# Taking row maxima off attention scores by 32-row products instead of 64-row products

## The chip, the cores and the metric

The kernel runs on one core of a Trainium2 chip. The metric is the device time of one execution in microseconds (us). TensorE does the matrix products, VectorE (DVE) the reductions, ScalarE (ACT) the exponentials, GpSimd (POOL) small elementwise work and indirect DMA, and SyncE (SP) issues most transfers. All numbers are float32.

## The reference

The input x is 2 sequences of 2048 tokens with 256 features. The reference is one attention layer, a layer norm, one mixing and mixture-of-experts layer, and a layer norm:

```
qkv = x @ qkv_w + qkv_b            # 16 heads of 16; q and k rotated by a table indexed by head
scores = einsum('bhqd,bhkd->bhqk', q, k) / 16 ** 0.5
out = einsum('bhqk,bhkd->bhqd', softmax(scores), v) @ out_w + out_b
x = layernorm(x + out)
n = layer_norm(x, g1, be1);  x = x + n + (n @ mix_w + mix_b)
n = layer_norm(x, g2, be2)
probs = softmax(n @ router_w);  combine = weights of the 2 best of 8 experts
y_e = silu(n @ w1[e] + b1[e]) @ w2[e] + b2[e]
x = layernorm(x_before_ffn + sum_e combine_e * y_e)   # layernorm adds its own input too
```

The change concerns the second line and the softmax: every row of scores has its maximum subtracted before the exponential.

## The kernel before

**Stages.** A leading stage (to about 95 us) makes q, k and v of the first sequence. The attention stage follows, to about 1720 us by the trace. The experts' products fill the rest: tokens are gathered in lists by expert and worked on in tiles of 256.

**Visits and steps.** Attention is a list of 32 visits `w`: 2 sequences, 4 blocks of 512 queries, 4 groups of 4 heads. A visit has 16 steps `kt`, one for each 128 keys, so there are 512 steps. A step handles 128 keys by 512 queries for 4 heads.

**Operands.** A head has only 16 features. To keep precision, q and k are split in a high and a low part, and the four combinations are stacked: one head takes 64 partitions (16 features by 4 parts). Tiles `km[w][pair]` and `qm[w][pair]` hold two heads each, one in partitions 0 to 63, the other in 64 to 127. A product of one head therefore uses 64 rows of the 128-row array, and two heads stand side by side in the array: the profile shows such products as form 64*128 (rows by columns). They run in pairs, at the same time.

**One step.** TensorE's instructions stand in the order in which the program issues them (`tc.manual_schedule` covers TensorE, ScalarE, VectorE and SyncE):

1. `scores(w, kt, 0)` and `scores(w, kt, 1)`: for each of the two pairs of heads, two score products (line 529) into two PSUM banks of the pool `ps_sc` (4 banks), then two products (line 538) that add minus the row maximum to the same banks. The maxima of all 4 heads are rows of `mrow[w]`, each as a high and a low part; `sel[pair]` is a 0/1 matrix that picks the two rows of a head. Both line-538 products have 64 rows, nearly all zeros. Four exponentials (line 544) follow on ScalarE, one for each bank.
2. `max_step(t + AHEAD, 0)`: half of the row maxima's work for a step that comes 18 steps later (`AHEAD`). `maxima` makes two score products of 64 rows (line 485), transposed, into banks of the pool `ps_mx`, and VectorE reduces each to a column of maxima (line 493). `ps_mx` has 3 banks, so each product needs the bank that was used three products before, and waits until VectorE has reduced that one.
3. `values` of the step before: 4 heads times 128*32 products (line 559), side by side in the array's columns. One such group appears as 8 matmul records, in two passes.
4. `work(1.0)`: a queue of small jobs, due by step number and not by time: projections of finished blocks, the router, the q, k and v of the second sequence, copies of finished outputs.
5. `max_step(t + AHEAD, 1)`: the second half of the maxima's work, two more line-485 products.

In the last 18 steps nothing is left for `maxima`, and items 2 and 5 are empty.

**After a visit's maxima.** `maxima_done` puts the 4 heads' maxima, as high and low parts, in 8 columns of `mt`; `rows_of` transposes that into `mrow[w]`. `make_sel` makes the selecting matrices once, in the leading stage.

Of the kernel before, what the change touches and what calls it, by code (L numbers as in the profile page):

```python
# [24 lines left out]
F32 = mybir.dt.float32  # L25
F32R = mybir.dt.float32r
I32 = mybir.dt.int32
AF = mybir.ActivationFunctionType
# [4 lines left out]
P = 128  # L33
# [30 lines left out]
def seq_postln_kernel(  # L64
# [16 lines left out]
    nc = tc.nc  # L81
# [7 lines left out]
    ident = cp.tile([P, P], F32, name="ident")  # L89
# [63 lines left out]
    with ExitStack() as actx:  # L153

        ep = actx.enter_context(tc.tile_pool(name="early", bufs=1))
        ap_ = actx.enter_context(tc.tile_pool(name="attn", bufs=1))
        dp = actx.enter_context(tc.tile_pool(name="stacks", bufs=1, space=bass.MemoryType.DRAM))
        ps_sc = actx.enter_context(tc.tile_pool(name="ps_sc", bufs=4, space=PSUM))
# [19 lines left out]


        mt = [ap_.tile([P, 4, P], F32, name=f"mt{i}", tag=f"mt{i}") for i in range(2)]  # L180
        sel = [ap_.tile([P, P], F32R, name=f"sel{i}", tag=f"sel{i}") for i in range(2)]
        x_in: dict = {}

        def load_x(b, tb):
# [88 lines left out]
        def make_sel():  # L273


            for p in range(2):
                t5 = ap_.tile([P, 1], F32, name="t5", tag="t5", bufs=2)
                nc.vector.tensor_add(
                    t5, ident[:, 2 * p : 2 * p + 1], ident[:, 2 * p + 1 : 2 * p + 2]
                )  # L280
                for at in (64 + 2 * p, 65 + 2 * p):
                    nc.vector.tensor_add(t5, t5, ident[:, at : at + 1])
                nc.vector.tensor_copy(sel[p], t5.to_broadcast([P, P]))

        def dense_bias():

# [21 lines left out]
        def later(steps, fn, cost=0.0, urgent=False):  # L308

            count[0] += 1  # L310
            heappush(todo[0 if urgent else 1], (now[0] + steps, count[0], cost, fn))

        def work(budget):
            for heap in todo:
                while heap and heap[0][0] <= now[0] and budget > 0:
                    _, _, cost, fn = heappop(heap)
                    fn()
                    budget -= cost
# [13 lines left out]
        def bank(name, *shape):  # L332

            if leading[0]:
                return ps_sc.tile([P, *shape], F32, name=name, tag="sc")
            return ps_mx.tile([P, *shape], F32, name=name, tag="mx")
# [162 lines left out]
        def maxima_done(w):  # L499

            m = mt[w % 2]
            nm = ap_.tile([P, 4, 4], F32, name="nm", tag="nm", bufs=2)
            nc.vector.tensor_reduce(nm, pm.pop(w), AX.X, ALU.max, negate=True)

            def part(t, low):
                return t.rearrange("p i (j k l) -> p i k j l", j=2, l=2)[:, :, 0:2, :, low]

            nmv = nm.rearrange("p i (k j) -> p i k j", j=2)
            nc.vector.tensor_single_scalar(
                part(m.bitcast(I32), 0), nmv.bitcast(I32), HIGH, ALU.bitwise_and  # L510
            )
            nc.vector.tensor_tensor(part(m, 1), nmv, part(m, 0), ALU.subtract)

            def rows_of():
                ps = bank("ps_m", 512)
                for i in range(4):
                    nc.tensor.transpose(ps[:, i * P : (i + 1) * P], m[:, i, :], ident)  # L517
                t = ap_.tile([P, 512], F32R, name=f"mrow_{w}", tag="mrow", bufs=2)
                nc.scalar.copy(t, ps)  # L519
                mrow[w] = t  # L520

            later(2, rows_of, 0.5, urgent=True)


        def scores(w, kt, pair):
            sc = [ps_sc.tile([P, 512], F32, name="ps_sc", tag="sc") for _ in range(2)]
            for j in range(2):
                r = slice(64 * j, 64 * j + 64)
                nc.tensor.matmul(  # L529
                    sc[j],  # L530
                    lhsT=km[w][pair][r, kt * P : (kt + 1) * P],
                    rhs=qm[w][pair][r, :],
                    start=True,
                    stop=False,
                )
            for j in range(2):
                r = slice(64 * j, 64 * j + 64)
                nc.tensor.matmul(  # L538
                    sc[j], lhsT=sel[pair][r, :], rhs=mrow[w][r, :], start=False, stop=True
                )  # L540
            out = []
            for j in range(2):
                ex = ap_.tile([P, 512], F32, name="ex", tag="ex", bufs=8)
                nc.scalar.activation(ex, sc[j], AF.Exp, scale=0.25)  # L544
                out.append(ex)
            return out

# [3 lines left out]
        def values(w, kt, exs):  # L551
            b, _, g = visits[w]
            if kt == 0:
                av_of[w] = ps_av.tile([P, 512], F32, name=f"av_{w}", tag="av")
            av = av_of[w]
            for h in range(4):

                at = 17 * (4 * g + h)
                nc.tensor.matmul(  # L559
                    av[32 * h : 32 * h + 32, :],  # L560
                    lhsT=vt[b][:, kt, at : at + 32],
                    rhs=exs[h],
                    start=(kt == 0),
                    stop=(kt == 15),
                )
            if kt == 15:
                attn_out(w)
# [497 lines left out]
        with tc.manual_schedule(engines=IN_ORDER):  # L1065

            ps = bank("ps_none", 512)
            for _ in range(4):
                nc.tensor.matmul(
                    ps,  # L1070
                    lhsT=mt[0][:, 0, :],
                    rhs=mt[0].rearrange("p i q -> p (i q)"),
                    start=True,
                    stop=True,
# [4 lines left out]
            for tb in range(TPB - 1):  # L1079
# [9 lines left out]
                if tb == 0:  # L1089
                    for c in range(2):  # L1090
                        nc.scalar.copy(wv[:, c], wr[:, c, :, 2, :])
            make_sel()


# [53 lines left out]
            def max_step(t, half):  # L1148
                if t < NSTEP:
                    maxima(t, half)  # L1150
# [15 lines left out]
            for t in range(NSTEP):  # L1166
                now[0] = t
                w, kt = divmod(t, 16)
                exs = scores(w, kt, 0) + scores(w, kt, 1)
                max_step(t + AHEAD, 0)  # L1170
                if before is not None:
                    values(*before)
                work(1.0)
                max_step(t + AHEAD, 1)
                before = (w, kt, exs)
# [159 lines left out]
    for n, o in enumerate(os_):  # L1335
        eng = nc.gpsimd if n % 2 == 0 else nc.vector
        mv = kp.tile([P, 4, 2], F32, name="mv", tag="mvz", bufs=4)
        for i in range(4):
# [3 lines left out]
        v, r, q, nb = (  # L1342
            kp.tile([P, 4], F32, name=k, tag=k, bufs=4) for k in ("vz", "rz", "qz", "nbz")
        )
# [3 lines left out]
        for i in range(4):  # L1348
# [5 lines left out]
                scale=r[:, i : i + 1],  # L1354
# [82 lines left out]
```

## Time and profile before

| | |
|---|---|
| median of the runs before | 2302.06 us (2300.25 to 2305.39, 3 runs) |
| the profiled execution | 2307.48 us, its span 2305.5 us |
| mean granted TensorE clock | 0.987 |
| TensorE matmul busy | 2229.3 us, 97% of the span |
| weight loads busy | 1326.4 us |
| VectorE busy | 1541.0 us, 67% |
| ScalarE busy | 1379.9 us, 60% |
| GpSimd busy | 477.4 us, 21% |

Busy shares are averages over stages that have different limits. Ends of matmuls are modelled, and matmuls are pipelined, so a record of 0.39 us may take only 0.23 us of TensorE's time: the distance between starts counts. In a view of the chain of waits, each piece is the time that one group of instructions adds to the chain that ended last. "Form" is rows by columns of the array that an instruction uses.

### The profile page before, as it was taken

Reading aid. Unit: us, or ns where it says so; the run is one execution under the profiler, and the core shown is the slowest. Engines: PE = TensorE matmul, PEld = TensorE weight load, DVE = VectorE, ACT = ScalarE, POOL = GpSimd, SP = SyncE. Lnnn points to the kernel's source line nnn. Section 1 sums busy time; section 2 is a strip of 40 time slices with the busy share of each in tenths; the row PEclk is TensorE's granted clock in tenths of the full one; section 3 lists DMA queues with packets and bytes.
Section 4 is the critical chain, followed back from the end, with each engine's and each line's share of the span. In section 5 each row is a group of like instructions: output and inputs, shape, how many; then the busy total and the mean of one; then the engine's idle time right before and its main releaser. Section 6 shows DMA issues by size and latency. Waiting matters only on the chain.

```text
span 2305.5 us, 39763 instructions
## 1 busy us (share of the span) xinstructions
PE 2229.3 (97%) x14186; PEld 1326.4 (58%) x14186; DVE 1541.0 (67%) x3108; ACT 1379.9 (60%) x2724; POOL 477.4 (21%) x838
## 2 busy tenths in 40 slices
PE   8999999999999999999999999999999999999993
PEld 3444555545555555555555555555547888888883
DVE  6788778778878888888888888888825211111114
ACT  2477667766777777677777767777773222223333
POOL 4111211240222112011111202112123322222113
PEclk8999999999999999999999999999999999999997
DMA  6733321232132111121111122111036777668994
GB/s 189 253 110 118 137 83 57 83 137 83 56 116 78 46 65 65 51 96 57 65 47 65 65 73 84 47 65 56 10 126 199 195 201 214 192 188 238 312 297 164
DMA packets 176757, 275.64 MB, mean 120 GB/s; under 512 B 22128, under 2 KB 107888, under 8 KB 176560
## 3 DMA queue, kind: packets, MB, share of 16 engines
q1 hardware_dynamic: 155600, 231.60, 30.4%
q0 software_dynamic: 20544, 40.59, 6.8%
q8 instruction: 112, 1.84, 0.3%
q10 hardware_dynamic: 416, 0.92, 0.1%
q14 instruction: 85, 0.70, 0.1%
HBM read 207.69 MB, written 62.74 MB: 117 GB/s over the span
## 4 chain that ended last, share of the span: by engine, by line
PE 88%; DVE 8%; DMA 2%; ACT 1%; issue 1%; POOL 0%; ACTq 0%; SPq 0%; DVEq 0%; POOLq 0%
PE av L559 21%; PE ps_mx L485 17%; PE ps_h L1264 11%; PE ps_y L1279 10%; PE ps_sc L538 9%; PE ps_sc L529 9%; DVE pm L493 4%; PE ps_qk L371 3%; PE ps_p L620 1%; PE ps_mix L620 1%; PE ps_v L429 1%; PE ps_o L581 1%; PE ps_m L517 1%; PE ps_l L799 1%; PE ps_x L1239 1%
## 5 line engine op out<-in xcount | busy, mean ns | idle before, releaser
L493 DVE TENSOR_REDUCE pm<-ps_mx 128x1 f32<-128x512 f32 x2048 | 1272.6, 681 | 193.0 <-PE ps_mx L485 185.2
L544 ACT ACTIVATE ex<-ps_sc 128x512 f32<-128x512 f32 x2048 | 1057.6, 603 | 353.5 <-PE ps_sc L538 340.2
L485 PE MATMUL ps_mx<-km,qm 64*128 64x512 f32 x2048 | 569.6, 470 | 22.7 <-DVE pm L493 21.5
L559 PE MATMUL av<-ex,vt 128*32 128x512 f32 x4096 | 546.4, 605 | 0.0
L485 PEld LDWEIGHTS ps_mx<-km,qm 64*128 64x128 f32 x2048 | 282.6, 183 | 457.9 <-DVE pm L493 345.0
L529 PE MATMUL ps_sc<-qm,km 64*128 64x512 f32 x2048 | 421.0, 394 | 0.0
L538 PE MATMUL ps_sc<-mrow,sel 64*128 64x512 f32 x2048 | 418.3, 392 | 0.7 <-ACT mrow L519 0.5
L1271 ACT ACTIVATE hT<-ps_h,b 128x256 f32<-128x256 f32 (+1 forms) x368 | 156.2, 425 | 364.0 <-PE ps_h L1264 356.0
L1264 PE MATMUL ps_h<-xT,w 128*128 128x256 f32 (+1 forms) x1472 | 274.5, 337 | 5.1 <-ACT hT L1271 2.7
L1279 PE MATMUL ps_y<-w,hT 128*128 128x256 f32 x1136 | 253.9, 379 | 1.7 <-DVE y L1289 1.7
L1264 PEld LDWEIGHTS ps_h<-xT,w 128*128 128x128 f32 x1472 | 226.7, 190 | 48.2 <-ACT hT L1271 21.0
L538 PEld LDWEIGHTS ps_sc<-mrow,sel 64*128 64x128 f32 x2048 | 204.8, 185 | 51.1 <-ACT mrow L519 9.6
L1279 PEld LDWEIGHTS ps_y<-w,hT 128*128 128x128 f32 x1136 | 212.0, 190 | 28.9 <-DVE y L1289 2.1
L529 PEld LDWEIGHTS ps_sc<-qm,km 64*128 64x128 f32 x2048 | 204.7, 185 | 37.1 <-ACT ex L544 14.4
L1243 DVE TENSOR_SCALAR xT<-ps_x,cols_sb 128x256 f32<-128x256 f32 (+1 forms) x92 | 40.2, 478 | 247.8 <-PE ps_x L1239 247.8
L1291 POOL DMA_INDIRECT acc<-y,xg x71 | 110.3, 1553 | 374.8 <-issue 134.5
L559 PEld LDWEIGHTS av<-ex,vt 128*32 128x32 f32 x4096 | 81.0, 108 | 130.2 <-issue 122.8
L1289 DVE TENSOR_TENSOR y<-ps_y,b 128x256 f32<-128x256 f32 x71 | 30.1, 423 | 176.2 <-PE ps_y L1279 170.8
L132 POOL TENSOR_SCALAR op_mul<-mv 128x4 f32<-128x4 f32 x18 | 4.2, 232 | 435.7 <-DVE mv L632 434.8
L371 PE MATMUL ps_qk<-xT,wqk 128*128 128x512 f32 x128 | 71.0, 668 | 2.2 <-ACT xT L355 2.2
L379 ACT ACTIVATE full<-ps_qk,bqk 128x512 f32<-128x512 f32 x32 | 22.0, 688 | 81.7 <-PE ps_qk L371 43.0
L387 POOL TENSOR_TENSOR full<-full,hi 128x512 f32<-128x512 f32 x27 | 34.4, 1276 | 175.3 <-DVE hi L383 170.6
(206 smaller groups left out, 1151.6 us busy)
## 6 DMA issues: line engine op xcount, KB each, us to landing
w<-in_w SPq DMA_DIRECT2D x92, 1024.0 KB
km<-st SPq DMA_DIRECT2D x248, 256.0 KB
qm<-st SPq DMA_DIRECT2D x62, 256.0 KB
st<-hi POOLq DMA_DIRECT2D x38, 256.0 KB
st<-full POOLq DMA_DIRECT2D x38, 256.0 KB
st<-hi SPq DMA_DIRECT2D x26, 256.0 KB
st<-full SPq DMA_DIRECT2D x26, 256.0 KB
xg<-x_list SPq DMA_DIRECT2D x25, 258.0 KB
```

Of the source, the lines that this page charges most:

```text
L371: nc.tensor.matmul(ps, lhsT=wqk[:, c, s, 8 * hh : 8 * hh + 8, :].rearrange("p h d -> p (h d)"), rhs=xT[b, tb][:, c, :], start=(c == 0), st ...
L485: nc.tensor.matmul(ps[j], lhsT=qm[w][pair][r, qt * P : (qt + 1) * P], rhs=km[w][pair][r, kb * 512 : (kb + 1) * 512], start=True, stop=True,)
L493: nc.vector.tensor_reduce(pm[w][:, qt, 2 * pair + j, kb : kb + 1], ps[j], AX.X, ALU.max)
L529: nc.tensor.matmul(sc[j], lhsT=km[w][pair][r, kt * P : (kt + 1) * P], rhs=qm[w][pair][r, :], start=True, stop=False,)
L538: nc.tensor.matmul(sc[j], lhsT=sel[pair][r, :], rhs=mrow[w][r, :], start=False, stop=True)
L544: nc.scalar.activation(ex, sc[j], AF.Exp, scale=0.25)
L559: nc.tensor.matmul(av[32 * h : 32 * h + 32, :], lhsT=vt[b][:, kt, at : at + 32], rhs=exs[h], start=(kt == 0), stop=(kt == 15),)
L620: nc.tensor.matmul(ps[:, i, :], lhsT=turned_in[:, c, at], rhs=w[:, c, :], start=(c == 0), stop=(c == 1),)
L1264: nc.tensor.matmul(ps, lhsT=w1t[:, c, k * P : (k + 1) * P], rhs=xT[:, c, :], start=(c == 0), stop=(c == 1),)
L1271: nc.scalar.activation(hT[:, k, :], ps, AF.Silu, bias=b1[:, k : k + 1])
L1279: nc.tensor.matmul(ps, lhsT=hT[:, k, s * P : (s + 1) * P], rhs=w2t[:, k, :], start=(k == 0), stop=(k == NFC - 1),)
L1291: nc.gpsimd.indirect_dma_start(out=acc, out_offset=bass.IndirectOffsetOnAxis(ap=xg[:, s, D : D + 1].bitcast(I32), axis=0), in_=y, in_offse ...
```

## The change

The four maximum products of a step get 32 rows each, a quarter of the array. Head h has its rows in partitions from 64 (h mod 2) + 32 (h div 2), and `mt` is laid out accordingly. One selecting matrix serves all heads. The eight products of a step are reordered, so that two 32-row products in one half of the array stand beside one 64-row score product in the other half. For head 2 the maximum comes first and the score is added to it. All four `ps_sc` banks of a step are taken by one call. The number of products, weight loads, exponentials and reductions stays the same.

```diff
-        sel = [ap_.tile([P, P], F32R, name=f"sel{i}", tag=f"sel{i}") for i in range(2)]
+        sel = ap_.tile([P, P], F32R, name="sel")
...
         def make_sel():
-            for p in range(2):
-                t5 = ap_.tile([P, 1], F32, name="t5", tag="t5", bufs=2)
-                nc.vector.tensor_add(
-                    t5, ident[:, 2 * p : 2 * p + 1], ident[:, 2 * p + 1 : 2 * p + 2]
-                )
-                for at in (64 + 2 * p, 65 + 2 * p):
-                    nc.vector.tensor_add(t5, t5, ident[:, at : at + 1])
-                nc.vector.tensor_copy(sel[p], t5.to_broadcast([P, P]))
+            t5 = ap_.tile([P, 1], F32, name="t5")
+            nc.vector.tensor_add(t5, ident[:, 0:1], ident[:, 1:2])
+            for at in range(32, P, 32):
+                for k in range(2):
+                    nc.vector.tensor_add(t5, t5, ident[:, at + k : at + k + 1])
+            nc.vector.tensor_copy(sel, t5.to_broadcast([P, P]))
...
             def part(t, low):
-                return t.rearrange("p i (j k l) -> p i k j l", j=2, l=2)[:, :, 0:2, :, low]
+                return t.rearrange("p i (j k l) -> p i k j l", j=2, k=2)[:, :, :, :, low]
...
-        def scores(w, kt, pair):
-            sc = [ps_sc.tile([P, 512], F32, name="ps_sc", tag="sc") for _ in range(2)]
-            for j in range(2):
-                r = slice(64 * j, 64 * j + 64)
+        def scores(w, kt):
+            sc = [ps_sc.tile([P, 512], F32, name="ps_sc", tag="sc") for _ in range(4)]
+
+            def product(h):
+                r = slice(64 * (h % 2), 64 * (h % 2) + 64)
                 nc.tensor.matmul(
-                    sc[j],
-                    lhsT=km[w][pair][r, kt * P : (kt + 1) * P],
-                    rhs=qm[w][pair][r, :],
-                    start=True,
-                    stop=False,
+                    sc[h],
+                    lhsT=km[w][h // 2][r, kt * P : (kt + 1) * P],
+                    rhs=qm[w][h // 2][r, :],
+                    start=h != 2,
+                    stop=h == 2,
                 )
-            for j in range(2):
-                r = slice(64 * j, 64 * j + 64)
+
+            def less(h):
+                at = 64 * (h % 2) + 32 * (h // 2)
+                r = slice(at, at + 32)
                 nc.tensor.matmul(
-                    sc[j], lhsT=sel[pair][r, :], rhs=mrow[w][r, :], start=False, stop=True
+                    sc[h],
+                    lhsT=sel[r, :],
+                    rhs=mrow[w][r, :],
+                    start=h == 2,
+                    stop=h != 2,
                 )
+
+            product(0)
+            product(1)
+            less(0)
+            less(2)
+            product(3)
+            product(2)
+            less(1)
+            less(3)
...
-                exs = scores(w, kt, 0) + scores(w, kt, 1)
+                exs = scores(w, kt)
```

More of the change, by code (lines that the diff above doesn't have):

```diff
@@ L522, in maxima_done @@
             later(2, rows_of, 0.5, urgent=True)
-        def scores(w, kt, pair):
-            sc = [ps_sc.tile([P, 512], F32, name="ps_sc", tag="sc") for _ in range(2)]
-            for j in range(2):
-                r = slice(64 * j, 64 * j + 64)
+        def scores(w, kt):
+            sc = [ps_sc.tile([P, 512], F32, name="ps_sc", tag="sc") for _ in range(4)]
+            def product(h):
+                r = slice(64 * (h % 2), 64 * (h % 2) + 64)
                 nc.tensor.matmul(
-                    sc[j],
-                    lhsT=km[w][pair][r, kt * P : (kt + 1) * P],
-                    rhs=qm[w][pair][r, :],
-                    start=True,
-                    stop=False,
-                )
-            for j in range(2):
-                r = slice(64 * j, 64 * j + 64)
+                    sc[h],
[3 more added lines that the diff above has]
+                    stop=h == 2,
+                )
+            def less(h):
+                at = 64 * (h % 2) + 32 * (h // 2)
+                r = slice(at, at + 32)
                 nc.tensor.matmul(
-                    sc[j], lhsT=sel[pair][r, :], rhs=mrow[w][r, :], start=False, stop=True
-                )
+                    sc[h],
[3 more added lines that the diff above has]
+                    stop=h != 2,
+                )
+            product(0)
[6 more added lines that the diff above has]
+            less(3)
             out = []
-            for j in range(2):
+            for h in range(4):
                 ex = ap_.tile([P, 512], F32, name="ex", tag="ex", bufs=8)
-                nc.scalar.activation(ex, sc[j], AF.Exp, scale=0.25)
+                nc.scalar.activation(ex, sc[h], AF.Exp, scale=0.25)
                 out.append(ex)
```

## The prediction

> **What bounds the kernel now.** I read the page first, then the chain of waits, then the timeline of one step. The page's bars:
>
> ```profile
> PE 2229.3 (97%) x14186; PEld 1326.4 (58%) x14186; DVE 1541.0 (67%) x3108; ACT 1379.9 (60%) x2724; POOL 477.4 (21%) x838
> ...
> L493 DVE TENSOR_REDUCE pm<-ps_mx 128x1 f32<-128x512 f32 x2048 | 1272.6, 681 | 193.0 <-PE ps_mx L485 185.2
> ...
> L485 PEld LDWEIGHTS ps_mx<-km,qm 64*128 64x128 f32 x2048 | 282.6, 183 | 457.9 <-DVE pm L493 345.0
> ...
> L538 PE MATMUL ps_sc<-mrow,sel 64*128 64x512 f32 x2048 | 418.3, 392 | 0.7 <-ACT mrow L519 0.5
> ```
>
> TensorE looks full, but the weight loads of L485 wait for VectorE's L493 (345.0 us), and L493 waits for L485 (185.2 us). The two engines hand three PSUM banks to and fro. What TensorE's time consists of is seen in the chain of waits between 1400 and 1440 us (start, us, what):
>
> ```profile
> 1405.63 0.35 PE ps_mx L485 x2
> 1405.98 0.99 PE av L559 x8
> 1406.98 0.43 PE ps_mx L485
> 1407.40 0.23 PE ps_sc L529
> 1407.64 0.23 PE ps_sc L538
> 1407.87 0.23 PE ps_sc L529 x2
> 1408.10 0.23 PE ps_sc L538 x2
> 1408.33 0.35 PE ps_mx L485 x2
> 1408.68 0.99 PE av L559 x8
> 1409.67 1.93 PE ps_mix L620 x8
> 1411.60 0.43 PE ps_mx L485 x2
> ...
> 1428.85 0.59 PE ps_m L517 x4
> 1429.43 1.73 PE ps_mix L620 x8
> ```
>
> Two things are to be seen. First, a pair of 64-row products costs one slot of 0.23 us, and a plain step is 0.43 + 4 x 0.23 + 0.35 + 0.99 = 2.69 us. Second, **a change of form costs 0.20 us.** L620 x8 takes 1.93 us behind L559 (form 128*32) but 1.73 us behind L517, which has L620's own form 128*128. L485 takes 0.43 us behind L559 and also behind L620, against 0.23 us for an equal pair behind its own form. From L620 to L485 only the rows differ, 128 against 64, and the price is the same 0.20 us.
>
> The remaining oddity is the L485 pair behind the scores: 0.35 us, not 0.23, with no change of form. The timeline of one step, in narrow windows, shows why:
>
> ```profile
> 902.84 0.69 DVE L493 TENSOR_REDUCE pm<-ps_mx 128x1 f32<-128x512 f32 x1 [0.21 <-issue]
> 903.34 0.40 PE L538 MATMUL ps_sc<-mrow,sel 64*128 64x512 f32 x2
> 903.57 0.51 PE L485 MATMUL ps_mx<-km,qm 64*128 64x512 f32 x2
> 903.59 0.18 PEld L485 LDWEIGHTS ps_mx<-km,qm 64*128 64x128 f32 x1
> ```
>
> The last weight load is that of the pair's second product. It starts 0.06 us after the reduction at 902.84 ends (902.84 + 0.69 = 903.53), because that reduction frees its bank. I followed this product through the trace: its load starts 0.05 us after that reduction's end in nine steps of ten and more. That reduction itself starts only when the L485 product ahead of the scores is done (start 902.31, 0.50 us long). So from one L485 pair to the next there is a path that doesn't touch the scores: 0.50 + 0.03 for the product, 0.69 for its reduction, 0.06 to the load, 903.59 - 902.31 = 1.28 us. TensorE's own path through the four score slots takes 903.57 - 902.31 = 1.26 us. **Shortening the scores alone gains 0.02 us a step at best.**
>
> **The change part by part.**
>
> *One slot removed.* With three slots, TensorE's path falls to 1.03 us and the bank path stays at 1.28. In the 494 steps that have maxima the gain is about 0: the L485 pair shows 0.58 us instead of 0.35. Only the last 18 steps, without maxima, could gain. They last 2.12 or 2.48 us in turn, 2.30 on average, the long ones held by exponentials (a score group of 0.59 in the rows under the rivals). A step can't be shorter there than four exponentials, 2.07 us by the timeline. That is 18 x 0.22 = 4 us.
>
> *Changes of form.* The new order on TensorE is L485, two 64-row scores, two 32-row products, two 64-row scores, two 32-row products, L485. If 32*128 is a form of its own, there are four changes where there was none. No run shows a 32-row product, so I bound the price: 0 if the quarters of the array work on beside a half, 0.20 us by the nearest row (L620 to L485, where only the rows change). Here a rule of the skill speaks against the change: "TensorEngine Tiling (Array Packing)", section "Key Properties", says that changing the tiling mode, not just the tile, drains the engine. Another speaks for it: "TensorE: Matmul & The Clock Gate", Part 3, "The mechanism", has masks of 32-row strips choose the place, so that products in different strips overlap. By the second the sum is 0 to -4 us. By the first nothing runs beside a product of another form, so all four slots remain and four changes come on top. The trace's 0.20 us at every change of form, of rows, of columns or of both, looks like the first: within one form weights are loaded ahead under the running product, at a change they are not. I take 0.20.
>
> The sum with drains: from the first score to the end of the L485 pair, the step was 4 x 0.23 + 0.35 = 1.27 us. It becomes 0.23 + 4 x 0.43 = 1.95 us. But the L485 pair no longer waits for its bank, and in many steps that wait was longer than in a plain one: between 1400 and 1440 us the pair's pieces behind scores are 0.36, 0.35, 0.35, 0.60, 0.58, 0.55, 0.36, 0.35, 0.53 and 0.57, mean 0.46, since VectorE's other work delays a reduction. With the mean, 1.95 - 0.92 - 0.46 = 0.57 us a step. 494 x 0.57 = 282 us. In the last 18 steps four groups of 0.43 and 0.99 make 2.71 us against 2.30: 18 x 0.41 = 7 us. Together **+289 us**.
>
> *What else moves.* ScalarE has four exponentials a step as before, 2.07 us, which fit in 2.7 and in 3.3 us. The bank waits of heads 2 and 3 stand one slot earlier; behind them on TensorE stand the other products of the step. In a plain step the last exponential ends at 905.43 and its bank's score would be due at 905.35 with three slots: 0.1 us, covered by the 0.35 us that the L485 pair would wait; with drains it is due later and waits for nothing. In the last 18 steps that cover is gone, and ScalarE is the bound used above. DMA queues (SP's and POOL's) are passed by nothing: no transfer moves, and small jobs are due by step number. `make_sel` has 8 small VectorE operations before and after, and `maxima_done` the same ones with other strides: 0. Experts' stage: 0.
>
> VectorE is late next if nothing drains (its reductions fill 2.48 of 2.69 us); with drains TensorE alone is the bound.
>
> The profiled execution took 2307.48 us (span 2305.5 and 2 us around it), so 2596 there. It lies 5.4 us above the median of the runs, so against that median: 2302 + 289 = **2591 us**.
>
> **The rivals.**
>
> *Quarters work beside halves; the slot is saved and lost to the bank wait.* For it: the array pairs unlike instructions in one form (in the last 18 steps a score of one head ran beside a maximum product of another). Against it: the 0.20 us at each change of rows. Time: 2302 - 4 = 2298 us, within 0.2%, or a little beyond where ScalarE lets the last steps run. This is the case that ends on the other side: one mechanism, the overlap of 32-row with 64-row products, in slots 2 and 3 of every step, priced at 0 per change. It decides when four changes cost less than the L485 pair's present wait plus the slot saved, 0.12 + 0.23 us, or 0.09 us each. The tail's rows, where alone it can gain:
>
> ```profile
> 1695.64 0.43 PE ps_sc L529 x2
> 1696.07 0.23 PE ps_sc L538
> 1696.30 0.59 PE ps_sc L529 x2
> 1696.89 0.23 PE ps_sc L538
> 1697.13 0.99 PE av L559 x8
> ```
>
> *Each half of the array changes by itself, or only part of the price falls due.* Then slots 2 and 3 and the L485 pair cost 0.43 each: 0.23 + 3 x 0.43 = 1.52, less 0.92 and 0.46, is 0.14 us a step, 71 us with the tail: about 2373. If all four slots remain and a change costs half, 0.10 us: 0.23 + 4 x 0.33 = 1.55, 0.17 us a step, about 2390. For it: weights of an idle strip might load early. Against it: no form change in the trace is cheaper than 0.20.
>
> **How the numbers follow.** Full drains: 0.62, with a range of its own from 2530 (0.17 us a change, all waits absorbed) to 2680 (0.20 us, and the plain step's 0.68 us everywhere, 494 x 0.68 + 7 = 343, and some 35 for dearer 32-row changes). Part of the price: 0.19. No drain: 0.19, of it 0.13 within 0.2% and 0.06 faster; 0.2%, 4.6 us, is about what a measurement of this kernel can tell from no change. Leaving the last case out would leave out the 0.19 and the ends of the first, over 2 in 10, so the range goes down to it: 2297 to 2680. The time given is that of full drains, 2591. Chances: faster 0.06, same 0.13, slower 0.81.
>
> **What would show it.** Right: in the chain, groups of L541 (32-row) and of L530 behind them at 0.43, L485 behind scores at 0.43 too with no wait for L493, plain steps of 3.37 us, VectorE's share lower. The last 18 steps at 2.7 us. Wrong: 32-row products starting within some ns of a 64-row score, three groups of 0.23, the L485 pair at 0.58 with the wait for L493 grown, and the step still 2.69 us. A step between would show which changes cost, and how much.

## The result, and the profile after

The changed kernel takes 2622.58 us (median of 4 runs, 2612.67 to 2647.66), the kernel before 2303.72 us in the same comparison (2300.25 to 2306.78). The ratio is 1.1401, 95% interval 1.1319 to 1.1483: 319 us slower. The prediction's time was 2591 us, from +289 us. One run below is left out of its ratio, the 2646.37 us of the changed kernel with halved reductions: its granted clock was 0.963, and it lies over 1.5% above the fastest run of that kernel.

The profiled execution took 2625.16 us, its span 2623.3 us. From its page: busy times, the granted clock by slices, and the groups that answer to those shown of before.

```profile
PE 2564.2 (98%) x14186; PEld 1249.3 (48%) x14186; DVE 1583.7 (60%) x3108; ACT 1435.8 (55%) x2724; POOL 477.8 (18%) x838
...
PEclk8999999999999998999999989999999999999997
...
L491 DVE TENSOR_REDUCE pm<-ps_mx 128x1 f32<-128x512 f32 x2048 | 1314.9, 684 | 462.9 <-PE ps_mx L483 429.0
...
L541 PE MATMUL ps_sc<-mrow,sel 32*128 32x512 f32 x2048 | 516.2, 500 | 0.7 <-ACT mrow L517 0.5
...
L483 PEld LDWEIGHTS ps_mx<-km,qm 64*128 64x128 f32 x2048 | 196.4, 186 | 481.7 <-DVE pm L491 382.2
...
L541 PEld LDWEIGHTS ps_sc<-mrow,sel 32*128 32x128 f32 x2048 | 191.5, 183 | 317.1 <-issue 307.2
```

TensorE's share of the span has hardly moved, 97 to 98%, and would tell nothing. The waits tell it: VectorE now stands idle for L483 for 429.0 us, up from 185.2 us, so VectorE waits for TensorE. The reverse wait must not be read from the 382.2 us that the weight loads of L483 show for L491 (345.0 before): 288 of them (251 before) stand ahead of the first load of the pair behind `values`, while TensorE is busy with L575 (L559 before), and by the median the bank had then been free for 1.56 us (0.88 before). The load that a reduction did hold up is the second one of the pair behind the scores. It starts within 0.08 us of the end of the reduction that frees its bank in 97% of the steps before and in 3% after, so that wait is off the path. And the weight loads of the 32-row products (L541) stand behind 307.2 us of "issue" idle time, 0.15 us for each of 2048: they wait for nothing that the profile shows. That is what a change of form looks like in this view.

The chain of waits of the profile after, a plain step (start, us, what):

```profile
1605.89 0.43 PE ps_mx L483
1606.31 0.23 PE ps_sc L530 x2
1606.55 0.42 PE ps_sc L541
1606.97 0.43 PE ps_sc L530 x2
1607.40 0.43 PE ps_sc L541 x2
1607.84 0.43 PE ps_mx L483 x2
1608.27 1.00 PE av L575 x8
```

Four groups now cost 0.43 us where before three of them cost 0.23 and one 0.35. The timeline of TensorE in the same step shows that nothing stands beside anything of another form:

```profile
1606.48 0.50 PE L541 MATMUL ps_sc<-mrow,sel 32*128 32x512 f32 x2
1606.91 0.49 PE L530 MATMUL ps_sc<-qm,km 64*128 64x512 f32 x2
1607.33 0.50 PE L541 MATMUL ps_sc<-mrow,sel 32*128 32x512 f32 x2
```

The third score product should have started within some ns of the two 32-row products at 1606.48, in the other half of the array. It starts 0.43 us later. So the three slots that were meant are four, as before, with four changes of form between them.

### The profile page after: what moved, and what is told of

Same layout as the page of the kernel before. It is cut to its first block, busy times and chain, and to the rows that moved or that the text cites. A ratio compares the mean times of both kernels' runs of the same rounds, so it can differ in the third digit from the quotient of the medians.

```text
span 2623.3 us, 39252 instructions
## 1 busy us (share of the span) xinstructions
PE 2564.2 (98%) x14186; PEld 1249.3 (48%) x14186; DVE 1583.7 (60%) x3108; ACT 1435.8 (55%) x2724; POOL 477.8 (18%) x838
## 4 chain that ended last, share of the span: by engine, by line
PE 94%; DVE 2%; DMA 2%; ACT 1%; issue 0%; POOL 0%; SPq 0%; ACTq 0%; DVEq 0%; POOLq 0%
PE av L575 20%; PE ps_mx L483 17%; PE ps_sc L541 17%; PE ps_sc L530 13%; PE ps_h L1280 9%; PE ps_y L1295 9%; PE ps_qk L369 2%; PE ps_p L636 1%; PE ps_mix L636 1%; PE ps_v L427 1%; PE ps_m L515 1%; PE ps_o L597 1%; DMA b<-in_b 1%; PE ps_l L815 1%; PE ps_x L1255 1%
## 5 line engine op out<-in xcount | busy, mean ns | idle before, releaser
L491 DVE TENSOR_REDUCE pm<-ps_mx 128x1 f32<-128x512 f32 x2048 | 1314.9, 684 | 462.9 <-PE ps_mx L483 429.0
L560 ACT ACTIVATE ex<-ps_sc 128x512 f32<-128x512 f32 x2048 | 1111.8, 597 | 605.1 <-PE ps_sc L541 604.9
L575 PE MATMUL av<-ex,vt 128*32 128x512 f32 x4096 | 558.3, 617 | 0.0
L483 PE MATMUL ps_mx<-km,qm 64*128 64x512 f32 x2048 | 526.2, 504 | 7.2 <-DVE pm L491 7.2
L541 PE MATMUL ps_sc<-mrow,sel 32*128 32x512 f32 x2048 | 516.2, 500 | 0.7 <-ACT mrow L517 0.5
L530 PE MATMUL ps_sc<-qm,km 64*128 64x512 f32 x2048 | 467.7, 451 | 0.0
L483 PEld LDWEIGHTS ps_mx<-km,qm 64*128 64x128 f32 x2048 | 196.4, 186 | 481.7 <-DVE pm L491 382.2
L541 PEld LDWEIGHTS ps_sc<-mrow,sel 32*128 32x128 f32 x2048 | 191.5, 183 | 317.1 <-issue 307.2
L530 PEld LDWEIGHTS ps_sc<-qm,km 64*128 64x128 f32 x2048 | 195.4, 187 | 138.1 <-issue 94.6
L575 PEld LDWEIGHTS av<-ex,vt 128*32 128x32 f32 x4096 | 81.6, 109 | 128.9 <-issue 127.6
```

The source lines that it names most:

```text
L483: nc.tensor.matmul(ps[j], lhsT=qm[w][pair][r, qt * P : (qt + 1) * P], rhs=km[w][pair][r, kb * 512 : (kb + 1) * 512], start=True, stop=True,)
L491: nc.vector.tensor_reduce(pm[w][:, qt, 2 * pair + j, kb : kb + 1], ps[j], AX.X, ALU.max)
L530: nc.tensor.matmul(sc[h], lhsT=km[w][h // 2][r, kt * P : (kt + 1) * P], rhs=qm[w][h // 2][r, :], start=h != 2, stop=h == 2,)
L541: nc.tensor.matmul(sc[h], lhsT=sel[r, :], rhs=mrow[w][r, :], start=h == 2, stop=h != 2,)
L560: nc.scalar.activation(ex, sc[h], AF.Exp, scale=0.25)
L575: nc.tensor.matmul(av[32 * h : 32 * h + 32, :], lhsT=vt[b][:, kt, at : at + 32], rhs=exs[h], start=(kt == 0), stop=(kt == 15),)
```

## The experiments

Ratios are to the kernel before, run in the same comparison on the same chip. The runs were made in two comparisons. In the first (rows alone, slot left out with whole and with halved reductions, maxima grouped) the kernel before had a median of 2301.80 us; in the second (the other four) it had 2313.93 us. The chip on record is the same, and why the medians lie 12 us apart is not known, so ratios and differences are compared, not times.

**Rows alone.** The order of before is kept, and only the rows of the maximum products are those of the change. In the changed kernel's `scores`:

```diff
-            less(0), less(2), product(3), product(2), less(1), less(3)
+            less(0), less(1), product(2), product(3), less(2), less(3)
```

and every bank's score comes first (start), its maximum second (stop).

> Maximum products of 32 rows as in the changed kernel, but in the old order: scores 0 and 1, maxima 0 and 1, scores 2 and 3, maxima 2 and 3, each bank's score first. Nothing stands beside a product of another form, and four slots are meant. Theory (each change between 64-row and 32-row products costs 0.20 us): four changes, first score to the end of the L483 pair 0.23 + 4 x 0.43 = 1.95 us, plain step 3.37 us, as in the changed kernel: 2600 to 2640 us. Rival (the new order, the maximum ahead of the score in head 2, or the earlier bank waits cost the time): within 0.5% of the kernel before, 2292 to 2315 us.

Measured: 2647.34 us, ratio 1.1515 (1.1485 to 1.1544). The chain has the changed kernel's pieces:

```profile
1353.62 0.43 PE ps_mx L483
1354.05 0.23 PE ps_sc L530
1354.28 0.43 PE ps_sc L541 x2
1354.71 0.43 PE ps_sc L530 x2
1355.14 0.42 PE ps_sc L541 x2
1355.57 0.43 PE ps_mx L483
1355.99 1.00 PE av L575 x8
```

The whole loss comes with the 32 rows. The new order, head 2's reversed sum and the earlier bank waits are not its cause. The median lies a little above the expected 2640 us; the last section says what moved it.

**Half the changes.** In the kernel before, only heads 2 and 3 get 32-row maximum products (rows 64 j to 64 j + 31 already hold their maxima):

```diff
-                r = slice(64 * j, 64 * j + 64)
+                r = slice(64 * j, 64 * j + (32 if pair == 1 else 64))
```

> The kernel before, with only the maximum products of heads 2 and 3 cut from 64 to 32 rows, in their place; those of heads 0 and 1 keep 64. Two changes of form a step, four slots. Theory (0.20 us a change, less the bank wait that they cover): 3 x 0.23 + 2 x 0.43 = 1.55 from the first score to the end of the L485 pair, against 1.27 plain and 1.38 mean: 494 x 0.17 = 84 us and about 5 in the last steps, 2380 to 2400 us; plain step 2.97 us. Rival (the changed kernel's loss comes from having all rows of 32, or from the order): about 2302 us. If a change cost 0.20 with nothing covered: 2302 + 512 x 0.40 = 2507 us.

Measured: 2424.37 us, ratio 1.0472 (1.0454 to 1.0491), that is +110 us against the kernel before beside it, where +78 to +98 was expected. The chain:

```profile
1354.42 0.43 PE ps_mx L485
1354.85 0.24 PE ps_sc L529 x2
1355.09 0.23 PE ps_sc L538 x2
1355.32 0.23 PE ps_sc L529 x2
1355.55 0.42 PE ps_sc L538 x2
1355.97 0.43 PE ps_mx L485 x2
1356.40 0.99 PE av L559 x8
```

The price appears exactly at the two places where a change of form was added, and at none of the others. The plain step is 2.98 us in the trace, 2.97 expected. Two changes cost 110 us and four 319, not twice 110: the first 0.12 us and more of each step is covered by the bank wait. But that cover was put too high. From the first load of one L485 pair to the second load of the next, across the scores, the traces have a mean of 1.40 us before and 1.62 us here: 0.22 us a step, where 0.17 was worked out. In 16% of the steps here the second load still starts right behind the reduction, so some of the wait is left.

**What a removed slot is worth.** The maximum products of heads 2 and 3 are left out of the kernel before:

```diff
-                    stop=False,
+                    stop=pair == 1,
...
-            for j in range(2):
+            for j in range(2 if pair == 0 else 0):
```

> The kernel before, without the two maximum products of heads 2 and 3 (their maxima are not subtracted): three slots a step, no change of form. It shows what the changed kernel would have had if the quarters had worked beside the halves. Theory (a path through three PSUM banks and one reduction, 1.28 us, bounds the stretch from L485 pair to L485 pair): the pair behind the scores takes 0.58 us and not 0.35, plain step still 2.69 us, only the last 18 steps gain: 2294 to 2302 us. Rival (TensorE's slots bound the step): 512 x 0.23 = 118 us less, 2186 us.

Measured: 2297.19 us, ratio 0.9982 (0.9973 to 0.9991), 4.6 us less. The chain shows where the slot went:

```profile
1355.94 0.43 PE ps_mx L485 x2
1356.37 0.23 PE ps_sc L529 x2
1356.60 0.23 PE ps_sc L538 x2
1356.83 0.23 PE ps_sc L529 x2
1357.06 0.58 PE ps_mx L485 x2
1357.64 1.00 PE av L559 x8
```

One group of 0.23 is gone, and the L485 pair behind the scores has grown from 0.35 to 0.58 us. Even if quarters did work beside halves, the change could by this have gained little more.

**That the reductions hold it.** Two kernels let L493 reduce half of each bank, `ps[j][:, 0:256]`, so that the maxima cover half the keys. The first keeps all slots, the second also leaves out the slot as above.

> The kernel before with each reduction of L493 reading 256 of its 512 columns (maxima over half the keys), all four slots kept. Theory (bank path): the L485 pair behind the scores falls from 0.35 us in a plain step and 0.46 on average to 0.23, so 494 x 0.12 = 59 to 494 x 0.23 = 114 us less: 2190 to 2245 us. Rival (reductions are off the path, TensorE's slots alone bound): 2295 to 2310 us.

Measured: 2221.87 us, ratio 0.9597 (0.9584 to 0.9611), 92 us less. A reduction now lasts 0.42 us, and the pair costs what any pair does:

```profile
1357.69 0.23 PE ps_sc L538 x2
1357.92 0.23 PE ps_mx L485 x2
1358.15 0.99 PE av L559 x8
```

> As e3_slot_left_out, and each reduction of L493 reads 256 of its 512 columns (maxima over half the keys). A reduction takes about 0.41 us, the bank path about 1.0 us, TensorE's path through three slots 1.03 us. Theory (bank path): now the slot counts, and the bank wait of 0.46 - 0.23 us goes too: 494 x 0.46 = 227 us at most, less where VectorE's other work or ScalarE is late: 2090 to 2150 us. Rival (slots alone): about 2186 us, as e3_slot_left_out would be by that rival.

Measured: 2143.05 us, ratio 0.9306 (0.9288 to 0.9324), 159 us less. The slot that was worth 4.6 us is worth 159 - 92 = 67 us once the reductions are short (from the two comparisons). With 512 x 0.23 = 118 us as the most, part of it is still lost to small waits; the chain has them as 0.26 to 0.28 us in the last two groups. So neither TensorE's slots nor the reductions alone bounded the step: two paths of 1.26 and 1.28 us lay side by side.

**The same edit where TensorE alone should bound.** The changed kernel with halved reductions.

> The changed kernel with each reduction of L491 reading 256 of its 512 columns (maxima over half the keys). Theory (with drains TensorE alone is the bound): next to nothing, 2595 to 2645 us, where the same edit takes 59 to 114 us off the kernel before. Rival (the reductions still hold the L483 pairs): 2510 to 2565 us.

Measured: 2612.89 us (2601.31 to 2646.37), ratio 1.1275 (1.1234 to 1.1317), against 1.1401 (1.1319 to 1.1483) for the changed kernel. The intervals touch at their ends. A per cent may have been gained; the 4% that the edit gave the kernel before was not. The reductions are off the path, as the 3% of second loads above say too.

**Fewer changes by grouping.** All scores first, then all four 32-row products:

```diff
-            less(0), less(2), product(3), product(2), less(1), less(3)
+            product(2), product(3), less(0), less(1), less(2), less(3)
```

> All four scores first, then all four 32-row maximum products together: two changes of form a step, not four, and three slots if four quarters work side by side. TensorE alone would need 0.23 + 0.23 + 0.43 + 0.43 = 1.32 us from the first score to the end of the L483 pair, as much as the kernel before with its bank wait (1.27 plain, 1.38 mean): 2300 to 2315 us. But no exponential can start before the maxima, and the last score can't start before the last exponential of the step before: 2.07 us of exponentials, about 0.15 to the score, 0.32 to the maxima, 0.53 to the first exponential are 3.07 us a step. Theory (drains and that loop): 2450 to 2530 us. Rival (a step is TensorE's time alone): 2300 to 2315 us. If 32-row products don't work four at a time, 2550 us and more.

Measured: 2429.30 us, ratio 1.0552 (1.0535 to 1.0570), below the range expected by theory, and far from the rival's. Two pieces of the chain and two rows of the timeline:

```profile
1352.91 0.43 PE ps_mx L483 x2
1353.34 0.84 PE ps_sc L530 x4
1354.18 0.43 PE ps_sc L541 x3
1354.61 0.43 PE ps_mx L483 x2
...
1358.35 0.46 PE ps_sc L530 x4
1358.81 0.43 PE ps_sc L541 x2
```

```profile
1353.68 0.18 PEld L530 LDWEIGHTS ps_sc<-qm,km 64*128 64x128 f32 x1 [0.31 <-ACT ex L560]
...
1354.11 0.50 PE L541 MATMUL ps_sc<-mrow,sel 32*128 32x512 f32 x4
```

Four 32-row products do share one slot: 0.43 us for all four, 0.23 and one change. But in plain steps the last score waits for the last exponential of the step before, and the four scores cost 0.84 us instead of 0.46. That makes 3.13 us a step in the trace. The expected loss was too high because it put the wait on every step. Where a small job stands in a step (at 1358.35, behind the router's products) the exponentials are done in time and it vanishes.

**The clock.** In the changed kernel's trace the granted clock falls to half for 75 us within the attention stage, against 3 us before. Each of its six stretches (behind the stage's first 5 us) begins within 2 us of the end of a group of the router's products (two of these groups start at 524.65 and 1018.60 us in the chain, and last 1.9 us each), so these were given out in two groups, a step apart:

```diff
-                ps = bank("ps_l", 4, E)
-                for i in range(4):
+                ps = bank("ps_l", 2, E)
+                for i in range(2):      # the second two come one step later
```

> The changed kernel, with the router's 16 small products (ps_l, 1.9 us together, 8 columns each) given out in two groups of 8, one step apart. In the changed kernel's trace TensorE's clock falls to half for 75 us within the attention stage, in stretches that begin right behind those groups; a plain step takes 5.3 us there, not 3.38. Theory (a thin group amid drains lets the clock fall): few or no such stretches, 75 x (1 - 3.38 / 5.3) = 27 us less, 2585 to 2605 us. Rival (drains alone let it fall, or it falls by chance): 2610 to 2650 us as the changed kernel.

Measured: 2617.50 us (2607.39 to 2630.81), ratio 1.1315 (1.1275 to 1.1356). Inconclusive in time, and against the theory in the trace: its profile still has 65 us at half clock within the stage, 44 of them in one stretch. Each of the four stretches again begins about 2 us behind router products, three of them behind a first half, which lasts 1.06 us. Splitting the group doesn't remove them. That the router's products set them off is likely by where they begin, but no run leaves these products out, and why some stretches last longer stays open.

The expectation's 5.3 us for a step at half clock was too short. The chain has 5.91 us, from 526.54 to 532.45:

```profile
524.65 1.89 PE ps_l L815 x16
526.54 0.72 PE ps_mx L483 x2
...
530.59 1.86 PE av L575 x8
532.45 0.97 PE ps_m L515 x4
```

No version here beats both kernels and still does the whole computation. The two that are faster by more than a quarter of a per cent take maxima over half the keys.

## Why the prediction was right

The range, 2297 to 2680 us, also held the case without any loss, so a result within it says little. What was tested is the time given for full drains, and the pieces of the step.

**The price of a change, 0.20 us: right.** It came from 128 to 64 rows, as no 32-row product had run. All four changes of the new order show it, in both directions between 64 and 32 rows. The plain step was given as 3.37 us; its median in the trace is 3.38. The last 18 steps were given as 2.71 us:

```profile
2020.60 1.00 PE av L575 x8
2021.59 0.43 PE ps_sc L530 x2
2022.03 0.42 PE ps_sc L541 x2
2022.45 0.43 PE ps_sc L530 x2
2022.89 0.42 PE ps_sc L541
```

**The rule of the Trainium skill that spoke against the change** ("TensorEngine Tiling (Array Packing)", "Key Properties": a changed tiling mode drains the engine) agrees with the trace, where a 32-row product even delays a 64-row product in rows that it doesn't use. How much of the 0.20 us is the drain, and how much the weight load of 0.18 us that no longer runs ahead, was not separated. The overlap of strips ("TensorE: Matmul & The Clock Gate", Part 3) holds within one form: four 32-row products shared a slot.

**The partial rivals: wrong.** Had each half of the array changed by itself, the stretch would be 1.52 us; it is 0.23 + 4 x 0.43 = 1.95.

**The bank wait: right.** A slot saved without any change of form gave 4.6 us, against 4 predicted, and left 0.58 us in the L485 pair, as written. The prediction also took the page's 345.0 us for this wait; most of it stands behind `values`, while TensorE is busy (the section on the result). The timeline of one step, not that figure, showed the path.

**The cover: right with four changes, too generous with two.** The term of 0.46 us for the L485 pair behind the scores was a mean over ten pieces of one 40 us stretch. Over all steps at full clock, the mean from the first load ahead of the scores to the second load behind them is 1.40 us before and 1.97 us after: 0.57 us, as summed. That a mean of ten pieces came so close is in part luck. With two changes the same term gave 84 us, 89 with the last steps, and the run 110. There the sum took all of the wait as covered, and 0.04 us a step of it was left at full clock (1.61 us), which is 494 x 0.04 = 20 us. The clock (24 us at half speed in its trace) may explain about 10 us more; the two are not separated.

**What the sum left out: the clock.** The sum took TensorE's clock as unchanged. At half clock a plain step takes 5.91 us and not 3.38, so 75 us of it cost about 75 x (1 - 3.38 / 5.91) = 32 us, an estimate, of about the size of the 30 us between +289 and +319. The changed kernel's runs scatter by 35 us, so the agreement is no closer than that.

## What to carry to other kernels

In these runs, small products shared a slot of the array only with products of one form. Before mixing forms, look in the chain of waits for what the next group costs behind another form and behind its own; here each change cost 0.20 us, nearly the 0.23 us of the slot to be saved. And before removing work from the busiest engine, follow a buffer from its writer to its reader and back: a path of 1.28 us through three banks stood beside TensorE's 1.26 us, so a whole slot was worth 0.2%.

## What was unexpected of the hardware

The granted clock fell although TensorE was recorded as busy throughout. Three stretches of the changed kernel, before, in and after such a fall (us, then busy us of TensorE with its instructions, weight loads, VectorE, ScalarE and GpSimd, then clock, DMA share and GB/s):

```profile
1000.00:1021.00 21.00, 21.00 (x136) 9.00 (x128) 13.78 (x23) 13.84 (x26) 1.04 (x1) 1.00 0.00 1
1021.00:1045.00 24.00, 24.00 (x85) 8.10 (x84) 12.82 (x31) 10.09 (x19) 0.25 (x1) 0.51 0.32 110
1045.00:1066.00 21.00, 21.00 (x127) 7.85 (x125) 15.71 (x28) 12.72 (x25) 13.42 (x37) 1.00 0.13 45
```

TensorE is busy for all of each stretch, by records, and at half clock does 85 instructions where it did 136. Time at half clock within the attention stage, one profile each: 0 to 10 us in the kernels without changes between 64 and 32 rows (before, slot left out, half reduced, both), 17 and 24 us with two changes a step, 48 to 75 us with four (rows alone, split router, changed kernel), and 129 us in the profile of the changed kernel with halved reductions, which no other reading here rests on. It goes with the number of changes of form; that these are its cause was not shown. Where it begins is plainer: behind the first 5 us of the stage, 32 of the 34 stretches of all profiles begin within 2.5 us of the end of a group of router products. Every kernel has seven such groups (the split one twice as many, of half the size), and the kernel before has one stretch, of 3.4 us. The fall goes with the wider scatter of these kernels too: the changed kernel's four runs have mean clocks of 0.980, 0.978, 0.975 and 0.964 and times of 2612.67, 2620.00, 2625.16 and 2647.66 us, in that order, and the four of the rows-alone kernel lie between 0.977 (2618.65 us) and 0.960 (2655.16 us), where the kernel before holds 0.984 to 0.988.
